# Experts 3 to 5 of a mixture of experts: the second product by seven block products, and its scaled additions and scatters moved into the next expert

## The chip, the cores and the metric

One core of a Trainium2 chip runs the whole program. The metric is the time of one execution on the device, in microseconds. The kernel before takes 1454.23 us, the median of three runs (1453.94 to 1454.76).

The engines have short names in the profile: PE is TensorE (PEld its weight loads), DVE is VectorE, ACT is ScalarE, POOL is GpSimd, SP is SyncE, which here issues DMAs.

## What is computed

The program is two transformer layers on 4096 tokens of width 256: gated attention in groups, a low-rank feed-forward, an attention with relu weights, and a mixture of experts. The change touches only the last. There, eight experts each choose their 1024 best tokens, and a token's output is the sum over the experts that chose it:

```
S = sigmoid(xt @ Wg).T
G, I = top_k(S, k)                       # 8 experts, k = 1024 tokens each
ex = xt[I]                               # gathered rows, 1024 x 256 per expert
hid = gelu(einsum('ekh,ehf->ekf', ex, W1) + b1)       # 1024 x 1024
out = (einsum('ekf,efh->ekh', hid, W2) + b2) * G[..., None]   # 1024 x 256
new_x = zeros.at[I].add(out)             # scattered back and added
```

The result then goes through a layer norm and is added to x. All is float32.

## The kernel before

The mixture of experts is a loop over 16 units `u` (line 2388), two for each expert `e`: `q` = 0 and 1 are the first and second 512 of its 1024 tokens. A unit's rows come as four gathered tiles of 128 tokens (`lists[e].got`), which TensorE transposes in `turn` into `xT[u]`, with the features in the partitions. The order of instructions on TensorE, VectorE and ScalarE is the program's own order (a manual schedule); on GpSimd it is left to the scheduler up to expert 5 and is the program's own from expert 6 on.

**The two ways to the hidden layer.** Experts 0, 1, 2 and 7 use `feed_forward`, once per unit: eight blocks of 128 hidden features, each two matmuls of 512 columns. Experts 3 to 6 (`by_seven`) use `feed_forward_by_seven`, both units at once. The 1024 tokens and the 1024 hidden features are each halved, and the product of 2 x 2 blocks is made from seven block products instead of eight (Strassen's method in Winograd's form). The loop over `f` runs over four chunks, each with seven matmuls of 512 columns into four banks named a to d, all under the tag "mm" with five banks. VectorE adds the partial products up in `u2`, `c22`, `c21` and `c12`, and four gelus of ScalarE write `hid`. The sums of weight blocks that these products need are made by `weight_sums` on GpSimd (four subtractions or additions of 128x512), those of tokens by `token_sums` on VectorE.

**The second product.** `project_back(u, hid)` makes a unit's four output tiles. For each, eight matmuls of 256 columns sum over the hidden features in a bank `py` (tag "y", two banks); then VectorE adds the bias and multiplies by the gates (lines 2332, 2333) and GpSimd scatters the tile with an adding indirect DMA into `acc_d` in DRAM (line 2334). The tile `y` has seven buffers. The scatters of an expert wait for all those of the expert before.

**What is fitted in between.** `turns_within(u)` says which transposes and token sums for the next units go behind which tile of `project_back`. Before an expert by seven, all transposes of both its units stand in the last unit of the expert before, behind tiles 0, 1 and 2.

The lists of chosen tokens for later experts are made beside all this. `agenda` holds their steps in order: for each list sort, rank, chunks, two steps of places, collect and gather. `go_on_with_lists(u, time, within)` is called at set points; it takes one step if the time booked for the last ones has run out and `u` is far enough, and with `within` only a step that has no TensorE work. `rank`, `chunks` and `places` are rows of small VectorE operations (lines 1916 to 1971); `gather` ends in eight row fetches on GpSimd (`got`, line 2005).

**The end.** In expert 6, `fetch_last` fetches the rows of the last expert's tokens into `xg` (eight more fetches), ahead of expert 6's second product in GpSimd's order. At the start of expert 7 `begin_last` reads `acc_d` back as soon as all scatters are done, and expert 7's units carry the last layer norm in `aside`, by a table (`beside_last`): statistics on VectorE, scaling on ScalarE, stores, and at the very end the final scatters of the chosen rows (line 2110). Its second products are added by line 2328.

Room that serves twice in the change: `wq1`, `wk1`, `wv` are the weights of the attention before, no longer needed here; `accg` and `xg` belong to expert 7.

Of the kernel before, what the change touches and what calls it, by code (L numbers as in the profile page):

```python
# [9 lines left out]
F32 = mybir.dt.float32  # L10
# [3 lines left out]
AF = mybir.ActivationFunctionType  # L14
ALU = mybir.AluOpType
# [4 lines left out]
P = 128  # L20
D = 256
DC = D // P
TB = 512
NJ = TB // P
# [13 lines left out]
FC = DFF // P  # L38
# [7 lines left out]
NE = 8  # L46
# [28 lines left out]
def kernel(  # L75
# [32 lines left out]
    nc = tc.nc  # L108
    B, S, _ = x_in.shape
    NT = B * S  # L110
# [1644 lines left out]
    with ExitStack() as st4:  # L1755
# [409 lines left out]
        QPE = NC // NJ  # L2165
        xT = {}

        def turn(u, c, half=None):

            if c == 0 and not half:  # L2170
                xT[u] = wk.tile([P, DC, TB], F32, tag="xT", name="xT")
            e, q = divmod(u, QPE)
            tiles = range(NJ) if half is None else range(half * NJ // 2, (half + 1) * NJ // 2)
            tp = ps.tile([P, NJ, P], F32, tag="mm", name="tp", bufs=5)
            for i in tiles:
                nc.tensor.transpose(tp[:, i, :], lists[e].got[q * NJ + i][:, c * P : (c + 1) * P], ident)
# [4 lines left out]
            copy = nc.scalar.copy if by_seven(e) else nc.vector.tensor_copy  # L2181
            copy(xT[u][:, c, cols], tp.rearrange("p j t -> p (j t)")[:, cols])  # L2182

        def by_seven(e):

            return 3 <= e < NE - 1

        rooms = [x.rearrange("p j d -> p (j d)")[:, h * TB : (h + 1) * TB] for x in xs[:4] for h in range(2)]
        seven = dict(zip(("sum0", "T1", "sum1", "T2", "T4", "S1", "S2", "S4"), rooms))
# [13 lines left out]
        def token_sums(e, n):  # L2203

            (b11, b21), (b12, b22) = ([xT[QPE * e + q][:, c, :] for c in range(DC)] for q in range(QPE))
            t1, t2, t4 = (seven[name] for name in ("T1", "T2", "T4"))
            dst, x, y = ((t1, b12, b11), (t2, b22, t1), (b12, b22, b12), (t4, b21, t2))[n]
            nc.vector.tensor_tensor(dst, x, y, ALU.subtract)

        def turns_within(u):  # L2210

            e, q = divmod(u, QPE)
            if u == QPE * NE - 1:
                return {}
            turns = {c: (lambda c=c: turn(u + 1, c)) for c in range(DC)}
            if q == QPE - 1 and by_seven(e + 1):
                both = [
                    turns[0], turns[1], lambda: turn(u + 2, 0), lambda: token_sums(e + 1, 0), lambda: turn(u + 2, 1),
                    *(lambda n=n: token_sums(e + 1, n) for n in (1, 2, 3)),
                ]  # L2220
                return {0: both[0:1], 1: both[1:4], 2: both[4:]}
            if by_seven(e) and q == 0:
                return {}
            return {2: [turns[0], turns[1]]} if u == 1 else {1: [turns[0]], 2: [turns[1]]}

        def feed_forward_by_seven(e):

            w1, w2 = weights[e]
            hid = [wk.tile([P, FC, TB], F32, tag="hid", name="hid") for _ in range(QPE)]
            (b11, b21), (t3, b22) = ([xT[QPE * e + q][:, c, :] for c in range(DC)] for q in range(QPE))  # L2230
            t1, t2, t4 = (seven[name] for name in ("T1", "T2", "T4"))
            half = DFF // 2
            s3 = w1[:, 0, half:DFF]
            s1, s2, s4 = (seven[name] for name in ("S1", "S2", "S4"))

            def product(bank, a, b, start, stop, f):
                nc.tensor.matmul(bank, lhsT=a[:, f * P : (f + 1) * P], rhs=b, start=start, stop=stop, skip_group_check=not start)  # L2237

            gelus = []

            def gelu(n, f, src):
                gelus.append(nc.scalar.activation(hid[n][:, f, :], src, AF.Gelu, bias=mb1[:, e * FC + f : e * FC + f + 1]))

            HC = FC // 2
            for f in range(HC):
                a, b, c, d = (ps.tile([P, TB], F32, tag="mm", name=f"ph{k}", bufs=5) for k in range(4))
# [5 lines left out]
                nc.vector.tensor_tensor(u2, u2, b, ALU.add)  # L2252
                product(c, s3, t3, True, True, f)
                nc.vector.tensor_tensor(c22, u2, c, ALU.add)
                product(d, s1, t1, True, True, f)
                nc.vector.tensor_tensor(c22, c22, d, ALU.add)
                product(a, w1[:, 1, 0:half], b21, False, True, f)
                gelu(0, f, a)
                if f < HC - 1:
                    go_on_with_lists(QPE * e, 3.2, True)  # L2260
                gelu(1, HC + f, c22)
                product(c, w1[:, 1, half:DFF], t4, False, True, f)
                nc.vector.tensor_tensor(c21, u2, c, ALU.add)
                gelu(0, HC + f, c21)
                product(d, s4, b22, False, True, f)
                nc.vector.tensor_tensor(c12, u2, d, ALU.add)
                gelu(1, f, c12)
                go_on_with_lists(QPE * e, 3.0)
            for q in range(QPE):
                if q == 0 and by_seven(e + 1):  # L2270
                    weight_sums(e + 1, gelus[-1])
                if q == 0 and e == NE - 2:
                    fetch_last()
                project_back(QPE * e + q, hid[q])

        def feed_forward(u):
            e, q = divmod(u, QPE)
# [30 lines left out]
        def project_back(u, hid):  # L2308

            e, q = divmod(u, QPE)  # L2310
            w1, w2 = weights[e]
            ahead = turns_within(u)
            for i in range(NJ):
                k = q * NJ + i
                py = ps.tile([P, D], F32, tag="y", name="py")
                for f in range(FC):
                    nc.tensor.matmul(  # L2317
                        py,
                        lhsT=hid[:, f, i * P : (i + 1) * P],
                        rhs=w2[:, f, :],  # L2320
                        start=(f == 0),
                        stop=(f == FC - 1),
                    )
# [9 lines left out]
                nc.vector.tensor_scalar(y, y, gates, None, ALU.mult)  # L2333
                scatter = nc.gpsimd.indirect_dma_start(  # L2334
                    out=acc_d[:, :],
                    out_offset=lists[e].at_chunk(k),
                    in_=y,
                    in_offset=None,
                    bounds_check=NT - 1,
                    oob_is_err=True,  # L2340
                    compute_op=ALU.add,
                )
# [91 lines left out]
```

## Time and profile before

The profiled execution took 1461.5 us; its span, from first to last instruction, is 1459.7 us. Below are the busy times of its last stages, in us; TensorE's granted clock is a share of full speed.

| stage (us from the start) | length | PE | DVE | ACT | POOL | PE clock |
|---|---|---|---|---|---|---|
| expert 3, 1169.5 to 1224.6 | 55.1 | 55.1 | 33.8 | 15.3 | 25.8 | 1.00 |
| expert 4, 1224.6 to 1279.6 | 55.0 | 55.0 | 27.4 | 15.4 | 25.8 | 1.00 |
| expert 5, 1279.6 to 1334.7 | 55.1 | 55.1 | 27.5 | 15.4 | 25.8 | 1.00 |
| expert 6, 1334.7 to 1393.8 | 59.1 | 56.0 | 24.1 | 13.2 | 30.4 | 0.97 |
| expert 7 and the end, 1393.8 to 1459.7 | 65.9 | 56.1 | 38.2 | 26.9 | 37.7 | 0.94 |

How to read it: TensorE's ends are modelled, so a busy TensorE need not be at its peak; what counts is whether it ever waits. A row of a timeline gives the start, the busy time, the engine, the line, the operation, its output and inputs, their shapes, and in brackets the idle time before it with what ended it. Each float32 matmul appears as two records, each with its own weight load.

### The profile page before, as it was taken

Reading aid. Unit: us, or ns where it says so; the run is one execution under the profiler, and the core shown is the slowest. Engines: PE = TensorE matmul, PEld = TensorE weight load, DVE = VectorE, ACT = ScalarE, POOL = GpSimd, SP = SyncE. Lnnn points to the kernel's source line nnn. Section 1 sums busy time; section 2 is a strip of 40 time slices with the busy share of each in tenths; the row PEclk is TensorE's granted clock in tenths of the full one; section 3 lists DMA queues with packets and bytes.
Section 4 is the critical chain, followed back from the end, with each engine's and each line's share of the span. In section 5 each row is a group of like instructions: output and inputs, shape, how many; then the busy total and the mean of one; then the engine's idle time right before and its main releaser. Section 6 shows DMA issues by size and latency. Waiting matters only on the chain.

```text
span 1459.7 us, 26465 instructions
## 1 busy us (share of the span) xinstructions
PE 1407.1 (96%) x10392; PEld 859.7 (59%) x10392; DVE 863.5 (59%) x2133; ACT 735.9 (50%) x1014; POOL 531.2 (36%) x662
## 2 busy tenths in 40 slices
PE   8999999999889999999999999949999999999997
PEld 4666666666644445454454547717666656756674
DVE  5457555666454637664757486885545766355246
ACT  4244454444368887878778788712221232232143
POOL 4123322322352223423333223413425325543655
PEclk9999999999999999999999999979999999999998
DMA  8400000001652373537244711152414223333365
GB/s 223 140 1 1 0 1 1 1 1 40 206 166 83 115 223 94 154 117 233 73 142 149 227 59 35 46 163 41 106 26 121 50 84 69 78 97 58 76 168 133
DMA packets 104853, 138.76 MB, mean 95 GB/s; under 512 B 25469, under 2 KB 64794, under 8 KB 104602
## 3 DMA queue, kind: packets, MB, share of 16 engines
q1 hardware_dynamic: 74512, 81.75, 18.2%
q0 software_dynamic: 30160, 55.32, 16.3%
q8 instruction: 81, 1.33, 0.4%
q14 instruction: 42, 0.34, 0.1%
q10 hardware_dynamic: 58, 0.01, 0.0%
HBM read 75.29 MB, written 61.51 MB: 94 GB/s over the span
## 4 chain that ended last, share of the span: by engine, by line
PE 86%; DVE 6%; issue 2%; DMA 2%; POOL 2%; ACT 1%; another core or an unknown queue 1%; SPq 0%; POOLq 0%; DVEq 0%; ACTq 0%
PE po L1553 16%; PE py L2317 14%; PE sc L1532 10%; PE ph L2237 7%; PE ph L2291 7%; PE pg L722 4%; PE pv L738 4%; PE py L848 3%; PE pt L1308 2%; PE pq L397 2%; PE po L820 2%; PE ph L904 2%; PE pv L431 2%; PE po L824 1%; PE pkv L835 1%
## 5 line engine op out<-in xcount | busy, mean ns | idle before, releaser
L1710 ACT ACTIVATE w<-sc 128x1024 f32<-128x1024 f32 x395 | 379.9, 1023 | 60.8 <-PE sc L1532 60.2
L1553 PE MATMUL po<-w,vaug 128*17 128x256 f32 (+1 forms) x4608 | 256.0, 358 | 1.5 <-DVE turned L1611 1.2
L2317 PE MATMUL py<-w,hid 128*128 128x256 f32 x1024 | 230.6, 382 | 3.1 <-DVE y L2332 3.1
L2317 PEld LDWEIGHTS py<-w,hid 128*128 128x128 f32 x1024 | 193.1, 191 | 33.5 <-issue 4.4
L1712 DVE TENSOR_SCALAR w<-sc 128x1024 f32<-128x1024 f32 x117 | 142.4, 1220 | 79.5 <-PE sc L1532 76.1
L1553 PEld LDWEIGHTS po<-w,vaug 128*17 128x17 f32 x4608 | 116.3, 97 | 118.0 <-issue 48.3
L1532 PE MATMUL sc<-q,kT 64*128 64x512 f32 (+1 forms) x1152 | 170.3, 404 | 2.5 <-ACT w L1710 1.3
L1532 PEld LDWEIGHTS sc<-q,kT 64*128 64x128 f32 x1152 | 89.9, 185 | 83.5 <-issue 46.7
L2334 POOL DMA_INDIRECT acc_d<-y,idx x56 | 88.1, 1574 | 119.8 <-DVE y L2333 59.5
L2298 ACT ACTIVATE hid<-ph,mb 128x512 f32<-128x512 f32 (+1 forms) x72 | 46.1, 640 | 164.8 <-PE ph L2291 137.2
L2291 PE MATMUL ph<-xT,w 128*128 128x512 f32 (+1 forms) x288 | 114.8, 552 | 0.3 <-DVE xT L2182 0.3
L2005 POOL DMA_INDIRECT got<-tok_d,idx x64 | 66.9, 1045 | 113.0 <-DVE idx L1995 96.0
L2291 PEld LDWEIGHTS ph<-xT,w 128*128 128x128 f32 x288 | 52.6, 190 | 51.3 <-issue 48.5
L371 POOL DMA_DIRECT2D kT<-k_d x32 | 23.4, 732 | 118.4 <-PE sc L1532 55.4
L2332 DVE TENSOR_TENSOR y<-py,mb 128x256 f32<-128x256 f32 x56 | 23.5, 420 | 71.8 <-PE py L2317 51.7
L722 PE MATMUL pg<-nT,wh 128*128 128x512 f32 x128 | 61.6, 613 | 1.5 <-ACT nT L661 1.5
L848 PE MATMUL py<-wo,oT 128*128 128x256 f32 x256 | 61.6, 384 | 0.0
L738 PE MATMUL pv<-wh,nT 128*128 128x512 f32 x128 | 59.7, 592 | 0.0
L848 PEld LDWEIGHTS py<-wo,oT 128*128 128x128 f32 x256 | 47.5, 190 | 17.6 <-issue 11.1
L746 ACT ACTIVATE v<-v 128x512 f32<-128x512 f32 x32 | 20.2, 630 | 62.7 <-DVE v L745 62.7
L1137 POOL TENSOR_TENSOR rsb<-veb,mhalf 128x1 f32<-128x1 f32 x30 | 19.6, 653 | 86.8 <-DVE veb L1136 86.8
L586 POOL TENSOR_TENSOR x<-x,y 128x1024 f32<-128x1024 f32 x13 | 30.6, 2355 | 56.3 <-ACT y L575 56.3
(352 smaller groups left out, 2338.0 us busy)
## 6 DMA issues: line engine op xcount, KB each, us to landing
q<-q_d POOLq DMA_DIRECT2D x16, 1024.0 KB
kT<-k_d POOLq DMA_DIRECT2D x32, 512.0 KB
w<-in_L_ffn_W_dram SPq DMA_DIRECT2D x16, 1024.0 KB
k_d<-parts SPq DMA_DIRECT2D x48, 256.0 KB
q_d<-parts SPq DMA_DIRECT2D x48, 256.0 KB
acc_d<-logits SPq DMA_DIRECT2D x8, 512.0 KB
tok_d<-hg SPq DMA_DIRECT2D x30, 128.0 KB
x<-in_L_attn_x_dram SPq DMA_DIRECT2D x7, 512.0 KB
```

The source lines that it names most:

```text
L722: nc.tensor.matmul(pg, lhsT=wh[:, c, HID + e * P : HID + (e + 1) * P], rhs=d["nT"][:, c, :], start=(c == 0), stop=(c == DC - 1),)
L738: nc.tensor.matmul(pv, lhsT=d["nT"][:, c, i * P : (i + 1) * P], rhs=wh[:, c, 0:HID], start=(c == 0), stop=(c == DC - 1),)
L848: nc.tensor.matmul(py, lhsT=d["oT"][:, e, :], rhs=wo[:, e, :], start=(e == 0), stop=(e == EC - 1))
L1532: nc.tensor.matmul(sc[:, j, m * n : (m + 1) * n], lhsT=row["kT"][t, r][rows, u, (kt + m) * P : (kt + m + 1) * P], rhs=row["q"][qh, t][rows ...
L1553: nc.tensor.matmul(po[rows : rows + HD + 1, at : at + n], lhsT=row["v"][:, kt + m, HQ * t + 4 * r + 2 * u + j, :], rhs=w[:, j, (2 * m + pa ...
L1710: nc.scalar.activation(w, sc, AF.Relu)
L1712: nc.vector.tensor_scalar(w, sc, 0.0, None, ALU.max)
L2005: return nc.gpsimd.indirect_dma_start(out=dst, out_offset=None, in_=rows[:, :], in_offset=self.at_chunk(c), bounds_check=NT - 1, oob_is_er ...
L2237: nc.tensor.matmul(bank, lhsT=a[:, f * P : (f + 1) * P], rhs=b, start=start, stop=stop, skip_group_check=not start)
L2291: nc.tensor.matmul(ph, lhsT=w1[:, c, f * P : (f + 1) * P], rhs=xT[u][:, c, h * n : (h + 1) * n], start=(c == 0), stop=(c == DC - 1),)
L2317: nc.tensor.matmul(py, lhsT=hid[:, f, i * P : (i + 1) * P], rhs=w2[:, f, :], start=(f == 0), stop=(f == FC - 1),)
L2334: scatter = nc.gpsimd.indirect_dma_start(out=acc_d[:, :], out_offset=lists[e].at_chunk(k), in_=y, in_offset=None, bounds_check=NT - 1, oob ...
```

## The change

`back_by_seven(e)` is true for experts 3, 4 and 5. For these, `project_back_by_seven` takes the place of both calls of `project_back`. It splits the 1024 tokens, the 1024 hidden features and the 256 outputs in halves and makes the second product from seven block products in five banks (p1, p4, p5, p6, p7; the second product on p1 and on p5 adds onto what is there). Each is 4 token tiles x 4 hidden blocks of matmuls with 128 columns, into one bank of tag "mm". The four sums of hidden blocks (s1 to s4, 128x2048 each) are made by VectorE; the four sums of W2's blocks by `back_sums` on GpSimd, behind chunk 0's last gelu of the same expert.

The bias times gate comes from ScalarE (`of_bias`); VectorE adds each gated half tile onto it (`add`). The first four half tiles are added at once; the other twelve half tiles' additions and all eight scatters go into `put_off`, twelve entries, of which six are taken at the end of each of the next expert's chunks. While `put_off` holds work the calls of `go_on_with_lists` in these chunks are left out. Within the second product three calls are left instead of eight.

The transposes for the next expert use the tag "y", whose banks are now 512 wide; `y` has nine buffers instead of seven.

```diff
-        def turn(u, c, half=None):
+        def turn(u, c, half=None, tag="mm"):
...
-            tp = ps.tile([P, NJ, P], F32, tag="mm", name="tp", bufs=5)
+            tp = ps.tile([P, NJ, P], F32, tag=tag, name="tp", bufs=5 if tag == "mm" else 2)
...
+        def back_by_seven(e):
+
+            return 3 <= e < NE - 2
...
-                if f < HC - 1:
+                if f < HC - 1 and (f > 1 or not put_off):
                     go_on_with_lists(QPE * e, 3.2, True)
...
-                go_on_with_lists(QPE * e, 3.0)
+                if f == 0 and back_by_seven(e):
+                    back_sums(e, gelus[-1])
+                if put_off:
+                    for _ in range(min(6, len(put_off))):
+                        put_off.pop(0)()
+                if not put_off:
+                    go_on_with_lists(QPE * e, 3.0)
+            if back_by_seven(e):
+                project_back_by_seven(e, hid)
+                return
...
+        def back_sums(e, behind):
+
+            (b11, b12), (b21, b22) = back_blocks(e)
+            t1, t2, t4 = (room.rearrange("p (f n) -> p f n", n=P) for room in back_rooms)
+            for dst, x, y in ((t1, b12, b11), (t2, b22, t1), (b12, b22, b12), (t4, b21, t2)):
+                after_all(nc.gpsimd.tensor_tensor(dst, x, y, ALU.subtract), [behind])
+
+        def project_back_by_seven(e, hid):
+
...
+            s1 = accg.rearrange("p k d -> p (k d)").rearrange("p (f t) -> p f t", t=TB)
+            s2, s3, s4 = a11, a21, a12
+            u2, v, c21, kept = (xg.rearrange("p k d -> p (k d)")[:, n * TB : (n + 1) * TB] for n in range(4))
+            ahead = turns_within(QPE * e + 1)
...
+            def lists_too(if_by_seven):
+                if not by_seven(e):
+                    go_on_with_lists(QPE * e + 1, 0.35)
+                elif if_by_seven:
+                    go_on_with_lists(QPE * e + 1, 3.5)
+
+            def product(bank, a, b, start, stop):
+                for i in range(NJ):
+                    for f in range(HC):
+                        nc.tensor.matmul(
+                            bank[:, i * P : (i + 1) * P],
+                            lhsT=a[:, f, i * P : (i + 1) * P],
+                            rhs=b[:, f, :],
...
+            def of_bias(q):
+                for k in range(q * NJ, (q + 1) * NJ):
+                    ys[k] = wk.tile([P, D], F32, tag="y", name="y", bufs=9)
+                    nc.scalar.activation(ys[k], mb2[:, e, :], AF.Identity, scale=gates[k])
+
+            def add(k, n, src):
+                i = k % NJ
+                y = ys[k][:, n * P : (n + 1) * P]
+                nc.vector.scalar_tensor_tensor(y, src[:, i * P : (i + 1) * P], gates[k], y, ALU.mult, ALU.add)
...
+            p1 = new_bank("p1")
+            product(p1, a11, b11, True, True)
+            nc.scalar.copy(u2, p1)
+            nc.vector.tensor_tensor(s1, a21, a22, plus)
+            nc.vector.tensor_tensor(s3, a11, a21, sub)
...
+            p4 = new_bank("p4")
+            product(p4, a22, t4, True, True)
+            nc.vector.tensor_tensor(s2, s1, a11, sub)
...
+            product(p1, a12, b21, False, True)
+            of_bias(0)
+            for k in range(NJ):
+                add(k, 0, p1)
+            summed_up = nc.vector.tensor_tensor(s4, a12, s2, sub)
+            if by_seven(e + 1):
+                weight_sums(e + 1, summed_up)
+            lists_too(True)
+            for do in ahead.get(0, ()):
+                do()
+            p5 = new_bank("p5")
+            product(p5, s1, t1, True, True)
+            nc.scalar.copy(kept, p5)
+            for do in ahead.get(1, ()):
+                do()
+            lists_too(True)
+            p6 = new_bank("p6")
+            product(p6, s2, t2, True, True)
+            nc.vector.tensor_tensor(u2, u2, p6, plus)
+            of_bias(1)
+            for do in ahead.get(2, ()):
+                do()
+            lists_too(True)
+            p7 = new_bank("p7")
+            product(p7, s3, t3, True, True)
+            nc.vector.tensor_tensor(v, u2, p7, plus)
+            nc.vector.tensor_tensor(c21, v, p4, plus)
+            nc.vector.tensor_tensor(v, v, kept, plus)
+            for k in range(NJ, NC):
+                put_off.append(lambda k=k: add(k, 0, c21))
+                put_off.append(lambda k=k: (add(k, 1, v), put(k)))
+            lists_too(False)
+            product(p5, s4, b22, False, True)
+            nc.vector.tensor_tensor(u2, u2, p5, plus)
+            put_off.extend(lambda k=k: (add(k, 1, u2), put(k)) for k in range(NJ))
...
-                py = ps.tile([P, D], F32, tag="y", name="py")
+                py = ps.tile([P, TB], F32, tag="y", name="py")[:, 0:D]
...
-                y = wk.tile([P, D], F32, tag="y", name="y", bufs=7)
+                y = wk.tile([P, D], F32, tag="y", name="y", bufs=9)
```

Here `a11` to `a22` are the halves of `hid` (first index tokens, second hidden features), `b11` to `b22` those of W2, `t1`, `t2`, `t4` the sums in `back_rooms` and `t3` the one that overwrites `b12`; `put(k)` is the scatter of tile k, as in `project_back`.

More of the change, by code (lines that the diff above doesn't have):

```diff
@@ L2180, in turn @@
             cols = slice(tiles[0] * P, (tiles[-1] + 1) * P)
-            copy = nc.scalar.copy if by_seven(e) else nc.vector.tensor_copy
+            copy = nc.scalar.copy if by_seven(e) or back_by_seven(e) else nc.vector.tensor_copy
             copy(xT[u][:, c, cols], tp.rearrange("p j t -> p (j t)")[:, cols])
@@ L2214, in turns_within @@
                 return {}
-            turns = {c: (lambda c=c: turn(u + 1, c)) for c in range(DC)}
+            tag = "y" if back_by_seven(e) else "mm"
+            turns = {c: (lambda c=c: turn(u + 1, c, tag=tag)) for c in range(DC)}
             if q == QPE - 1 and by_seven(e + 1):
                 both = [
-                    turns[0], turns[1], lambda: turn(u + 2, 0), lambda: token_sums(e + 1, 0), lambda: turn(u + 2, 1),
+                    turns[0], turns[1], lambda: turn(u + 2, 0, tag=tag), lambda: token_sums(e + 1, 0),
+                    lambda: turn(u + 2, 1, tag=tag),
                     *(lambda n=n: token_sums(e + 1, n) for n in (1, 2, 3)),
@@ L2221, in turns_within @@
                 return {0: both[0:1], 1: both[1:4], 2: both[4:]}
-            if by_seven(e) and q == 0:
+            if (by_seven(e) or back_by_seven(e)) and q == 0:
                 return {}
@@ L2274, in feed_forward_by_seven, with back_blocks @@
                 project_back(QPE * e + q, hid[q])
+        put_off = []
+        back_rooms = [x.rearrange("p c d -> p (c d)") for x in (wq1, wk1, wv)]
+        def back_blocks(e):
+            w2 = weights[e][1]
+            return [[w2[:, h * FC // 2 : (h + 1) * FC // 2, n * P : (n + 1) * P] for n in range(2)] for h in range(2)]
+        def back_sums(e, behind):
[3 more added lines that the diff above has]
+                after_all(nc.gpsimd.tensor_tensor(dst, x, y, ALU.subtract), [behind])
@@ new lines, in project_back_by_seven, with new_bank, put @@
+        def project_back_by_seven(e, hid):
+            (b11, t3), (b21, b22) = back_blocks(e)
+            t1, t2, t4 = (room.rearrange("p (f n) -> p f n", n=P) for room in back_rooms)
+            HC = FC // 2
+            (a11, a12), (a21, a22) = ([hid[q][:, h * HC : (h + 1) * HC, :] for h in range(2)] for q in range(QPE))
+            s1 = accg.rearrange("p k d -> p (k d)").rearrange("p (f t) -> p f t", t=TB)
+            s2, s3, s4 = a11, a21, a12
+            u2, v, c21, kept = (xg.rearrange("p k d -> p (k d)")[:, n * TB : (n + 1) * TB] for n in range(4))
+            ahead = turns_within(QPE * e + 1)
+            gates = [lists[e].got[k][:, D + e : D + e + 1] for k in range(NC)]
+            ys = {}
+            def new_bank(name):
+                return ps.tile([P, TB], F32, tag="mm", name=name, bufs=5)
+            def lists_too(if_by_seven):
[10 more added lines that the diff above has]
+                            rhs=b[:, f, :],
+                            start=start and not i and not f,
+                            stop=stop and f == HC - 1,
+                            skip_group_check=True,
+                        )
+            def of_bias(q):
[6 more added lines that the diff above has]
+                nc.vector.scalar_tensor_tensor(y, src[:, i * P : (i + 1) * P], gates[k], y, ALU.mult, ALU.add)
+            def put(k):
+                scatter = nc.gpsimd.indirect_dma_start(
+                    out=acc_d[:, :],
+                    out_offset=lists[e].at_chunk(k),
+                    in_=ys[k],
+                    in_offset=None,
+                    bounds_check=NT - 1,
+                    oob_is_err=True,
+                    compute_op=ALU.add,
+                )
+                after_all(scatter, scattered[e - 1] if e else ())
+                beside_each_other(scatter, scattered[e])
+            sub, plus = ALU.subtract, ALU.add
+            p1 = new_bank("p1")
[7 more added lines that the diff above has]
+            nc.vector.tensor_tensor(s2, s1, a11, sub)
+            lists_too(False)
+            product(p1, a12, b21, False, True)
[29 more added lines that the diff above has]
+                put_off.append(lambda k=k: (add(k, 1, v), put(k)))
+            lists_too(False)
+            product(p5, s4, b22, False, True)
+            nc.vector.tensor_tensor(u2, u2, p5, plus)
+            put_off.extend(lambda k=k: (add(k, 1, u2), put(k)) for k in range(NJ))
+            lists_too(False)
```

## The prediction

> **What bounds the kernel now.** I read the page's first part, then the TensorE timeline of experts 3 to 6, then the other engines' timelines at the places where the change works.
>
> ```profile
> PE 1407.1 (96%) x10392; PEld 859.7 (59%) x10392; DVE 863.5 (59%) x2133; ACT 735.9 (50%) x1014; POOL 531.2 (36%) x662
> ```
>
> TensorE sets the time. Its timeline (start, duration, engine, line, operation, output and inputs, count) shows expert 4's second product:
>
> ```profile
> 1250.07 17.43 PE L2317 MATMUL py<-w,hid 128*128 128x256 f32 x80
> 1267.34 0.60 PE L2176 MATMUL tp<-ident,got 128*128 128x128 f32 x4
> 1267.78 3.62 PE L2317 MATMUL py<-w,hid 128*128 128x256 f32 x16
> ```
>
> No idle bracket: 80 matmuls in 17.27 us, 0.216 us each. Experts 3, 4 and 5 take 55 us each, TensorE busy throughout. A matmul saved is time saved, and a wait added is time lost.
>
> **The product itself.** The 64 matmuls of an expert are 128 records (the page has x1024 for eight experts), 128 x 0.216 = 27.6 us. Seven products of 16 matmuls are 224 records with 128 columns. The nearest row has the same shape on both sides:
>
> ```profile
> 173.17 0.38 PE L820 MATMUL po<-packed,v 128*128 128x128 f32 x2
> 173.40 0.39 PE L824 MATMUL po<-head,kv 128*128 128x128 f32 x2
> ...
> 174.74 0.39 PE L824 MATMUL po<-head,kv 128*128 128x128 f32 x2
> 174.96 1.06 PE L688 MATMUL psim<-head,head 128*128 128x128 f32 x8
> ```
>
> From 173.17 to 174.96 lie 16 records, each with its own weight load: 0.112 us each. 224 x 0.112 = 25.1 us, so 2.5 us less per expert, **-7.6 us** for three. The Trainium skill (TensorE: Matmul & The Clock Gate, Back-to-back issue gap) speaks against this: in a stream of weight-load and matmul pairs the load is part of the spacing, about 81 ns at 128 columns against 56 for a matmul alone. Scaled by 1.45 a record would take 0.162 us, the product 36.3 us, and the change would lose 8.7 us per expert, 26 in all. The trace has the very pairs at 0.112, and I take the trace. Ends: 0.109 (transposes, 4 in 0.44 us) for -9.6 us, and 0.162.
>
> **What lies beside the products.** Count from the first of the seven. Each takes 3.58 us. VectorE gets four 128x2048 sums; 512 wide go at 0.61 us, 1024 wide at 1.14, so some 2.2 each: s1 is there at 3.9, s3 at 6.1, s2 at 8.4; p5 needs s1 at 11.2, p6 needs s2 at 15.7. s4, behind the first four additions, is ready at 14.1 and wanted at 23.3. With five 128x512 additions (3.0) and 16 half-wide scaled ones (4.2) VectorE gets 16 us per expert and loses 8 x 0.77 = 6.2; it was busy 10.6 of 29.5 us here. ScalarE gets two copies (0.57) and eight Identity rows (0.5, the rate at L2071), 5.1 us, where it was busy 3.7 of 29.5. I cost these at nothing; TensorE hides them. Without that cover the sum needed next (2.2 us) would show. The transposes stay 16; they come earlier, at 10.7 and 15.2 instead of 17.3. In expert 3 the gather of rows already stands at the end of the first product: row fetches start 1.2 us behind it, one per 1.32 us, the last issued at 11.6, and DMA traffic of that burst is over by 13.1. Four rows are wanted at 10.7, eight at 15.2: two microseconds to spare, cost nothing; per microsecond later, one lost. The two py banks are as many as before; y's nine buffers hold eight rows and one more. The eight scatters (1.85 us each on GpSimd when they queue) move into the next expert's chunks: with back_sums' 5.6 us they fill GpSimd from about 7.5 to 28 us of experts 4 and 5, and the next row fetches begin at 27 to 28, so the margin above loses at most one. SyncE's weight loads wait for the same last readers as before.
>
> **Put-off additions.** In the first product a chunk takes 6.01 us, and its sixth matmul pair overwrites a bank that VectorE must have read. This is chunk 0 of expert 4:
>
> ```profile
> 1226.16 1.28 DVE L1971 TENSOR_TENSOR at<-lo,each 128x1024 bf16<-128x1024 bf16 x2
> 1227.36 0.68 DVE L2252 TENSOR_TENSOR x<-x,ph 128x512 f32<-128x512 f32 x1
> 1228.15 0.69 DVE L2254 TENSOR_TENSOR hid<-x,ph 128x512 f32<-128x512 f32 x1
> ```
>
> L2252 starts 2.8 us into the chunk, L2254 ends at 4.29, the pair starts at once. So VectorE may be free for L2252 as late as X = 2.8; later costs X - 2.8. A half-wide scaled addition is not in the trace. The same operation goes at 0.17 us for 32 columns and 0.395 for 256, on a line between 0.26 for 128; six are 1.6 us, behind the chunk's own last addition (ends at 0.8). Chunk 1: X = 2.4, no loss. At the end of chunk 1 `put_off` is empty and the list work starts again, 1.2 us of places: chunk 2 has X = 3.6, 0.85 us lost. Chunk 0 lost 0.25 before (6.26 us), and that goes. Net 0.6 in experts 4, 5, 6: **+1.8 us**. Ends: 0 and 4.
>
> **back_sums on GpSimd.** These are four more 128x512 sums per expert behind chunk 0's last gelu. The row to read is expert 2, where weight_sums ran beside VectorE's search:
>
> ```profile
> 1154.63 4.52 DVE L1824 TENSOR_TENSOR ge<-by_e,tried 128x224 bf16<-128x224 f32 x4
> ```
>
> ```profile
> 1154.70 1.45 POOL L2201 TENSOR_TENSOR x<-w 128x512 f32<-128x512 f32 x1 [12.81 <-ACT hid L2298]
> 1156.23 1.30 POOL L2201 TENSOR_TENSOR w<-w 128x512 f32<-128x512 f32 x1
> ```
>
> Elsewhere these four VectorE operations take 1.30 us (at 1151.09), here 4.52: each waits out one sum on GpSimd, some 1.4 us. Now chunk 1 of expert 3:
>
> ```profile
> 1177.11 0.25 DVE L1927 SCALAR_TENSOR_TENSOR chosen<-upto,room,kinds 128x32 f32<-128x32 f32 x1
> 1177.39 0.19 DVE L1928 TENSOR_TENSOR chosen<-chosen,kinds 128x32 f32<-128x32 f32 x1
> ...
> 1178.17 0.68 DVE L2252 TENSOR_TENSOR x<-x,ph 128x512 f32<-128x512 f32 x1
> ```
>
> ScalarE's second gelu ends at 1177.17, so back_sums starts at about 1177.3. Three or four small operations with both inputs in SBUF stand from L1928 on; each waits, and L2252 moves from 1178.17 to 1181.7 or 1182.8. L2254 ends 1.5 later; the sixth pair stood at 1179.95. That is 3.3 to 4.4 us; I take **+3.8**. Ends: 0 and 6, since the one gap of this length in the trace (3.13 us at 1370.7) was followed by a granted clock of 0.5 and cost 5.1 in all. In experts 4 and 5 the put-off additions meet the sums: if these go first, two additions wait and chunk 1 has X = 4.7, 2 us lost; if a scatter goes first, chunk 2 gets one to two such waits, 1 to 2.6. I take 1.7 each, **+3.4**; ends 0 and 8.
>
> **Lists later, and the tail.** While `put_off` holds work the list steps stand still; gather moves from the end of chunk 1 to the end of chunk 3, 12 us. In expert 6 GpSimd then has 16 fetches before the scatters. They stood like this:
>
> ```profile
> 1369.17 1.01 POOL L2005 DMA_INDIRECT xg<-x_d,idx  x1 [0.30 <-issue]
> 1370.48 1.62 POOL L2334 DMA_INDIRECT acc_d<-y,idx  x1 [0.30 <-issue]
> ...
> 1395.05 1.55 POOL L2334 DMA_INDIRECT acc_d<-y,idx  x1 [1.32 <-DVE y L2333]
> 1399.70 1.08 POOL L2005 DMA_INDIRECT accg<-acc_d,idx  x1 [3.09 <-DMA acc_d<-y,idx]
> ```
>
> From the first fetch (1349.29) to the first scatter are 21.2 us. Starting 1.2 us into the second product, scatters begin at 22.4; at 1.85 us each (the spacing at 1215 to 1221) the eighth is issued at 35.3. The product lasts 28.5, so that is 6.8 us into expert 7, where it was 1.3: 5.5 later. The read-back waits for it, then stats, scales, stores, the second read-backs (1418.7, 1421.7) and their stats (1427.48). From there to L2328 at 1439.58 VectorE has 12.1 us with 1.6 of idle, so L2328 comes 4 us late, and the final row of reciprocals and scatters on GpSimd, 1441.01 to 1454.8, has hardly a gap to catch up in. **+4.2**; ends 0 and 6.
>
> **Sum.** -7.6 + 1.8 + 3.8 + 3.4 + 4.2 = +5.6 us. The profiled execution took 1461.5 us (span 1459.7), 7.3 above the median of 1454.23; 5.1 of that is one stall of expert 6, where VectorE waited 7.65 us for something the trace calls remote. The change touches nothing that explains it, so I count it as the profile's own and add the sum to the median: **1459.8 us**.
>
> **Rivals.** First, the products alone come through: GpSimd's sums find other moments, and expert 7's slack takes the delay. For it: TensorE without one gap, and POOL busy 36%. Against it: the row of 4.52 us. -7.6 + 1.8 = 1448.4, or 1452.6 with the late tail. Second, the weight load sets the pace: +26 and the waits, 1480 or more; against it 16 pairs at 0.112, for it only that the longest such run in the trace is short. Third, the rows for the next expert land late and TensorE waits in all three: two microseconds of margin used up and 2 to 4 more lost each time, 1466 to 1472.
>
> **Numbers.** Forecast with its near values (1456 to 1465) 0.55; first rival 0.20; a sum near zero, where one of the three waits fails to appear, 0.14; the third rival 0.08; the weight load 0.03. A measurement tells 0.2% (2.9 us) from no change. Faster 0.20, same 0.14, slower 0.66. The range takes in most of the first rival and stops short of the second and most of the third: 1449 to 1467.
>
> **What would show it.** The new matmuls 0.11 us apart, 25 us for each expert's seven products; gaps of 3 to 4 us in chunk 1 of expert 3, of 1 to 2 in chunks 1 and 2 of experts 4 and 5; VectorE's small operations stretched over back_sums; the last scatter of expert 6 some 7 us into expert 7; L2328's row behind VectorE in the last half expert. I am wrong if VectorE and back_sums hardly meet, or if expert 7 ends as far behind expert 6 as before.

## The result and the profile after

The changed kernel takes **1477.83 us** (median of four runs, 1475.82 to 1483.25), the kernel before 1454.09 beside it (1452.92 to 1454.76): a ratio of 1.017, interval 1.0142 to 1.0198. It is 23.7 us slower, where 5.6 were forecast; the range ended at 1467. The page of the profile after has

```profile
PE 1405.3 (95%) x10680; PEld 862.7 (58%) x10680; DVE 908.2 (62%) x2160; ACT 749.4 (51%) x1044; POOL 566.2 (38%) x674
```

TensorE's busy time hardly changed (1407.1 before: fewer matmuls, some of them at a lower clock), though its span is 16.9 us longer: what came is mostly waiting. The view of waits, TensorE alone, from 1160 us to the end (what was waited for, us in total, times, longest) gives nearly all of it:

```profile
PE ph L2243 <- DVE hid L2260: 12.0, 4, 4.5
PE tp L2176 <- DMA got<-tok_d,idx: 6.5, 7, 1.2
...
```

Neither line existed before. The first is the first product waiting for VectorE, the second the transposes waiting for the next expert's rows. A table of stages, from the starts in TensorE's timeline, places them; the other rows are the experiments below ("first" and "second" are the two products of an expert, in us, for experts 3, 4, 5 and 6).

| kernel | first product, 3 / 4 / 5 / 6 | second product, 3 / 4 / 5 / 6 | median us | before, same chip | ratio (95%) |
|---|---|---|---|---|---|
| before | 25.4 / 25.5 / 25.6 / 25.5 | 29.6 / 29.5 / 29.5 / 33.6 | 1454.09 | | |
| after | 29.9 / 31.2 / 31.8 / 26.2 | 29.9 / 29.9 / 29.9 / 28.6 | 1477.83 | 1454.09 | 1.0170 (1.0142–1.0198) |
| vector_sums | 25.4 / 26.2 / 26.2 / 26.2 | 31.5 / 31.6 / 31.6 / 34.3 | 1467.92 | 1457.57 | 1.0072 (1.0054–1.0090) |
| lists_on_time | 29.8 / 30.5 / 30.6 / 26.3 | 29.9 / 26.9 / 26.9 / 31.8 | 1472.42 | 1457.57 | 1.0114 (1.0088–1.0141) |
| in_pieces | 28.2 / 31.6 / 31.6 / 26.2 | 27.0 / 27.0 / 27.2 / 35.6 | 1468.60 | 1457.57 | 1.0084 (1.0056–1.0113) |
| all_three | 25.4 / 26.3 / 26.3 / 26.3 | 28.7 / 26.9 / 26.9 / 33.4 | 1456.96 | 1457.57 | 0.9994 (0.9984–1.0005) |
| sums_late | 25.4 / 26.2 / 26.2 / 26.2 | 30.0 / 33.2 / 33.2 / 35.0 | 1470.67 | 1456.41 | 1.0097 (1.0076–1.0119) |
| late_gpsimd | 25.4 / 25.5 / 25.5 / 25.5 | 27.0 / 34.9 / 32.2 / 35.7 | 1467.14 | 1456.41 | 1.0067 (1.0052–1.0082) |
| spread_vector | 25.4 / 25.8 / 25.5 / 25.5 | 27.0 / 28.7 / 28.7 / 35.4 | 1458.24 | 1456.41 | 1.0001 (0.9991–1.0011) |
| three_nine | 25.4 / 25.5 / 25.5 / 25.5 | 27.0 / 28.7 / 27.5 / 36.8 | 1457.75 | 1460.19 | 0.9978 (0.9967–0.9988) |
| fetch_between | 25.4 / 25.5 / 25.5 / 25.5 | 27.0 / 27.5 / 27.6 / 28.5 | 1452.61 | 1460.19 | 0.9957 (0.9943–0.9970) |
| fetch_between_again | 25.4 / 25.5 / 25.5 / 25.5 | 27.0 / 27.5 / 28.6 / 28.5 | 1452.78 | 1454.35 | 0.9989 (0.9982–0.9996) |
| before_between | 25.4 / 25.5 / 25.5 / 25.5 | 29.6 / 29.5 / 29.5 / 28.5 | 1455.56 | 1454.35 | 1.0007 (0.9999–1.0016) |

The kernel before differs by about 6 us between chips, so times are compared within a row only. A stage without a wait repeats between profiles to a tenth; expert 6's second product does not, and is taken up at the end of the experiments.

**The first product of expert 3.** VectorE's timeline (start, us, engine, line, operation, operands) beside GpSimd's four new sums, as in the prediction's fence of before, where L1928 took 0.19 and L2252, now L2258, started at 1178.17:

```profile
1176.69 1.17 DVE L1928 TENSOR_TENSOR chosen<-chosen,kinds 128x32 f32<-128x32 f32 x1
1177.89 0.19 DVE L1931 SCALAR_TENSOR_TENSOR place<-place,chosen 128x32 f32<-128x32 f32 x1
1178.12 1.13 DVE L1933 TENSOR_SCALAR hi<-place 128x32 f32<-128x32 f32 x1
1179.28 1.20 DVE L1935 SCALAR_TENSOR_TENSOR lo<-hi,place 128x32 bf16<-128x32 f32 x1
1180.40 0.68 DVE L2258 TENSOR_TENSOR x<-x,ph 128x512 f32<-128x512 f32 x1
```

```profile
1176.55 1.26 POOL L2305 TENSOR_TENSOR wq<-w 128x512 f32<-128x512 f32 x1 [4.07 <-ACT hid L2248]
...
1180.39 1.26 POOL L2305 TENSOR_TENSOR wv<-w,wk 128x512 f32<-128x512 f32 x1
```

Three operations of 0.2 us each take 1.1 to 1.2, one for each of the first three sums. L2258, which reads PSUM, keeps its 0.68 us although the fourth sum runs beside it. This is the mechanism that the prediction expected here.

**The first product of expert 5.** Here the put-off additions meet the same sums. VectorE's and then GpSimd's timeline:

```profile
1296.50 1.66 DVE L2349 SCALAR_TENSOR_TENSOR y<-xg,got,y 128x128 f32<-128x128 f32 x6
...
1302.51 5.40 DVE L2349 SCALAR_TENSOR_TENSOR y<-xg,got,y 128x128 f32<-128x128 f32 x6
1307.82 1.28 DVE L1971 TENSOR_TENSOR at<-lo,each 128x1024 bf16<-128x1024 bf16 x2
1309.03 0.68 DVE L2258 TENSOR_TENSOR x<-x,ph 128x512 f32<-128x512 f32 x1
```

```profile
1301.13 1.57 POOL L2352 DMA_INDIRECT acc_d<-y,idx  x1 [0.17 <-issue]
1302.22 1.78 POOL L2305 TENSOR_TENSOR wk<-w,wq 128x512 f32<-128x512 f32 x1
1303.45 1.76 POOL L2305 TENSOR_TENSOR w<-w 128x512 f32<-128x512 f32 x1
1304.67 1.75 POOL L2305 TENSOR_TENSOR wv<-w,wk 128x512 f32<-128x512 f32 x1
```

Six additions take 1.66 us in chunk 0 and 5.40 in chunk 1: 3.74 us more for three sums, 1.25 each. A scatter, gated by the additions, stands between the first sum and the other three, so these three move out of chunk 1's middle to the end of its work on VectorE, just where the second six additions are. Then a list step (1.28) follows, and L2258 starts 7.3 us into chunk 2 (1301.70) instead of the 2.8 it can afford. TensorE's timeline shows what that costs:

```profile
1305.13 1.02 PE L2243 MATMUL ph<-xT,w 128*128 128x512 f32 x2
1310.55 2.08 PE L2243 MATMUL ph<-x,w 128*128 128x512 f32 x2 [4.40 <-DVE hid L2260]
1312.42 1.91 PE L2243 MATMUL ph<-xT,x 128*128 128x512 f32 x2
...
1315.30 1.13 PE L2243 MATMUL ph<-xT,w 128*128 128x512 f32 x2
```

4.40 us of waiting, and then two pairs 1.87 and 1.84 us apart instead of 0.86 and 0.95: the granted clock of this stage is 0.89. The gap costs another 1.9 us after it is over.

**The seven products.** TensorE's timeline in expert 3:

```profile
1198.71 3.82 PE L2332 MATMUL p<-w,hid 128*128 128x128 f32 x32
1202.36 3.74 PE L2332 MATMUL p<-wv,hid 128*128 128x128 f32 x32
...
1210.26 3.74 PE L2332 MATMUL p<-wq,accg 128*128 128x128 f32 x32
1213.84 0.82 PE L2176 MATMUL tp<-ident,got 128*128 128x128 f32 x6
1215.86 0.33 PE L2176 MATMUL tp<-ident,got 128*128 128x128 f32 x1 [1.21 <-DMA got<-tok_d,idx]
1217.19 0.33 PE L2176 MATMUL tp<-ident,got 128*128 128x128 f32 x1 [1.00 <-DMA got<-tok_d,idx]
```

A product is 32 records in 3.57 to 3.65 us, 0.112 each: the row at L820 carried over. But the second eight transposes, 0.9 us of work, last from 1213.84 to 1217.35. GpSimd's fetches of those rows, and VectorE's sums of hidden blocks beside them:

```profile
1201.33 2.27 POOL L2005 DMA_INDIRECT got<-tok_d,idx  x1 [0.31 <-issue]
1203.89 1.97 POOL L2005 DMA_INDIRECT got<-tok_d,idx  x1 [0.30 <-issue]
1206.17 2.09 POOL L2005 DMA_INDIRECT got<-tok_d,idx  x1 [0.30 <-issue]
1208.56 1.01 POOL L2005 DMA_INDIRECT got<-tok_d,idx  x1 [0.30 <-issue]
...
1211.19 2.79 POOL L2005 DMA_INDIRECT got<-tok_d,idx  x1 [0.30 <-issue]
```

```profile
1200.36 2.29 DVE L2368 TENSOR_TENSOR accg<-hid 128x2048 f32<-128x2048 f32 x1 [0.71 <-ACT hid L2248]
1202.68 2.29 DVE L2369 TENSOR_TENSOR hid<-hid 128x2048 f32<-128x2048 f32 x1
1205.08 2.29 DVE L2373 TENSOR_TENSOR hid<-accg,hid 128x2048 f32<-128x2048 f32 x1
...
1210.82 2.28 DVE L2379 TENSOR_TENSOR hid<-hid 128x2048 f32<-128x2048 f32 x1
```

A fetch with no wide sum beside it takes 1.01 us. The four long ones end 0.95, 0.89, 0.89 and 0.88 us after the end of the sum that ran when they began (1203.60 against 1202.65, and so on): they stand still for the sum and then take their usual time. So the lock works both ways. The last fetch is issued at 1214.29, 15.6 us after the first product's end, where the prediction had 11.6.

**Expert 6 and the tail.** GpSimd's timeline, with expert 7 beginning at 1406.12:

```profile
1399.94 1.62 POOL L2470 DMA_INDIRECT acc_d<-y,idx  x1 [0.30 <-DVE xT L2182]
...
1413.00 1.55 POOL L2470 DMA_INDIRECT acc_d<-y,idx  x1 [0.31 <-issue]
1417.63 1.08 POOL L2005 DMA_INDIRECT accg<-acc_d,idx  x1 [3.07 <-DMA acc_d<-y,idx]
```

The last scatter is issued 6.9 us into expert 7 (forecast 6.8). Expert 7 takes 58.0 us instead of 56.1, and 12.6 us instead of 9.8 follow TensorE's last matmul.

### The profile page after: what moved, and what is told of

The parts are those of the page before. It is cut to its first block, busy times and chain, and to the rows that moved or that the text cites. A ratio compares the mean times of both kernels' runs of the same rounds, so it can differ in the third digit from the quotient of the medians.

```text
span 1476.6 us, 27151 instructions
## 1 busy us (share of the span) xinstructions
PE 1405.3 (95%) x10680; PEld 862.7 (58%) x10680; DVE 908.2 (62%) x2160; ACT 749.4 (51%) x1044; POOL 566.2 (38%) x674
## 4 chain that ended last, share of the span: by engine, by line
PE 80%; DVE 7%; issue 4%; DMA 4%; POOL 3%; ACT 1%; SPq 0%; POOLq 0%; ACTq 0%; DVEq 0%
PE po L1553 15%; PE sc L1532 10%; PE py L2453 7%; PE ph L2243 6%; PE ph L2427 6%; PE p L2332 4%; PE pg L722 4%; PE pv L738 4%; PE py L848 3%; PE pt L1308 2%; PE pq L397 2%; PE po L820 2%; PE ph L904 2%; PE pv L431 2%; PE po L824 1%
## 5 line engine op out<-in xcount | busy, mean ns | idle before, releaser
L1710 ACT ACTIVATE w<-sc 128x1024 f32<-128x1024 f32 x395 | 379.9, 1024 | 60.7 <-PE sc L1532 60.0
L2453 PE MATMUL py<-w,hid 128*128 128x256 f32 x640 | 143.9, 381 | 1.3 <-ACT hid L2434 0.7
L2453 PEld LDWEIGHTS py<-w,hid 128*128 128x128 f32 x640 | 119.6, 190 | 20.7 <-issue 3.0
L2005 POOL DMA_INDIRECT got<-tok_d,idx x64 | 82.0, 1281 | 87.2 <-DVE idx L1995 70.1
L586 POOL TENSOR_TENSOR x<-x,y 128x1024 f32<-128x1024 f32 x13 | 30.6, 2355 | 56.3 <-ACT y L575 56.3
```

The costliest lines, as they stand in the source:

```text
L1710: nc.scalar.activation(w, sc, AF.Relu)
L2005: return nc.gpsimd.indirect_dma_start(out=dst, out_offset=None, in_=rows[:, :], in_offset=self.at_chunk(c), bounds_check=NT - 1, oob_is_er ...
L2453: nc.tensor.matmul(py, lhsT=hid[:, f, i * P : (i + 1) * P], rhs=w2[:, f, :], start=(f == 0), stop=(f == FC - 1),)
```

## The experiments

**Theory**: GpSimd and VectorE keep each other out whenever both work on SBUF alone. GpSimd's four sums stop VectorE in the first product; VectorE's four wide sums stop the row fetches in the second. **Rival**: VectorE has simply too much to do, and the rows are late because their gather was moved.

**vector_sums**, the sums of W2's blocks on the other engine:

```diff
-                if f == 0 and back_by_seven(e):
-                    back_sums(e, gelus[-1])
...
             if back_by_seven(e):
+                back_sums(e)
                 project_back_by_seven(e, hid)
...
-            for dst, x, y in ((t1, b12, b11), (t2, b22, t1), (b12, b22, b12), (t4, b21, t2)):
-                after_all(nc.gpsimd.tensor_tensor(dst, x, y, ALU.subtract), [behind])
+            for dst, x, y in ((t1, b12, b11), (t2, b22, t1), (t4, b21, t2), (b12, b22, b12)):
+                nc.vector.tensor_tensor(dst, x, y, ALU.subtract)
```

> The four sums of W2's blocks (back_sums) go from GpSimd, behind chunk 0's last gelu, to VectorE, ahead of the seven products. Theory (the sums on GpSimd hold off VectorE's operations that read and write only SBUF): the first products of experts 3, 4 and 5, now 29.9, 31.2 and 31.8 us, return to 25.5 to 26.2 us, no gap of over 1 us stays in them, and the whole falls by 14 to 16 us, to about 1463. Rival (VectorE simply has too much to do once the put-off additions are there): the gap in expert 3 goes, 4.4 us, since nothing is put off there; the gaps of 4.5 us in chunk 2 of experts 4 and 5 stay; about 1473.

The first products fell to 25.4, 26.2 and 26.2 us. VectorE does the same additions and more, so the rival falls: sums on GpSimd cost 4.5, 5.0 and 5.6 us, and the put-off additions by themselves 0.7 us (one gap of 0.66 in chunk 2). TensorE's waits in this profile:

```profile
PE tp L2176 <- DMA got<-tok_d,idx: 7.3, 6, 1.5
PE py L2452 <- DVE y L2467: 3.8, 1, 3.8
PE ph L2243 <- DVE hid L2260: 2.0, 3, 0.7
```

The time stayed above the forecast. The second products take 1.6 us more each: their waits for rows grew by only 0.3 us each (the last fetch is issued 15.6 us in, as in the change), but behind each pair of waits the granted clock fell to 0.50 for 3.4 us, where it had stayed at 1.00. And expert 6 has a wait of its own.

**lists_on_time**, the list steps no longer held back:

```diff
-                if f < HC - 1 and (f > 1 or not put_off):
+                if f < HC - 1:
...
-                if not put_off:
-                    go_on_with_lists(QPE * e, 3.0)
+                go_on_with_lists(QPE * e, 3.0)
```

> The list steps are no longer held back while put-off additions are left. Theory (the late gather is what costs the seven products their gain in experts 4 and 5, and what lengthens the tail): the rows of experts 5 and 6 are fetched during the first product, the transposes' waits (2.1 us and a slow stretch, 2.9 in all) stay in expert 3 and go in 4 and 5: -6; the tail -3 to -4; the list steps in chunks 0 and 1 give 1 to 3 back: 1468 to 1471. Rival (VectorE is the bound in these chunks): the steps meet GpSimd's sums together with the put-off additions and each waits its 1.3 us: what is won is lost, 1477 or more.

The second products of experts 4 and 5 fell by 3.0 us to 26.9, expert 3's stayed, and expert 7 is back at 56.1. The first products gained 0.7 and 1.2. As the theory had it, one or two microseconds above its range. (The slow stretch that it counts in expert 3 is not there: the granted clock of the change's second products is 1.00.) In experts 4 and 5 three fetches each still meet wide sums (1.9 to 2.1 us), but the gather starts earlier and its last fetch is issued 11.2 us in, in time.

**in_pieces**, the same sums cut in four:

```diff
+            def in_pieces(dst, x, y, op):
+                for f in range(HC):
+                    last = nc.vector.tensor_tensor(dst[:, f, :], x[:, f, :], y[:, f, :], op)
+                return last
...
-            nc.vector.tensor_tensor(s1, a21, a22, plus)
+            in_pieces(s1, a21, a22, plus)
```

and so for s2, s3 and s4.

> The four sums of hidden blocks (s1 to s4) are made as four 128x512 pieces each instead of one 128x2048 operation. Theory (a fetch on GpSimd waits for the end of VectorE's running operation, so fetches of 2.0 to 2.8 us are ones that met a sum of 2.3 us): with pieces of 0.6 to 0.7 us a fetch takes 1.0 to 1.6 us, the rows land 3 to 4 us earlier, the waits of 2.2 us at the transposes go in experts 3, 4 and 5; -6 to -9, about 1470. Rival (VectorE's operations back to back keep GpSimd out as long as they follow each other, whatever their length): the fetches stay as long as the four pieces together, no change.

GpSimd's fetches in expert 3:

```profile
1197.04 1.46 POOL L2005 DMA_INDIRECT got<-tok_d,idx  x1 [0.31 <-issue]
1198.80 1.45 POOL L2005 DMA_INDIRECT got<-tok_d,idx  x1 [0.30 <-issue]
1200.56 1.50 POOL L2005 DMA_INDIRECT got<-tok_d,idx  x1 [0.31 <-issue]
1202.37 1.01 POOL L2005 DMA_INDIRECT got<-tok_d,idx  x1 [0.30 <-issue]
```

About 1.5 instead of 2.0 to 2.3; the last fetch is issued 12.1 us in instead of 15.6, and no transpose waits. The seven products take 27.0 us in all three experts, with gathers still late: a late gather costs nothing where the fetches do not meet wide sums, and in lists_on_time meeting them cost nothing where the gather was early. (A first piece also needs only the first hidden blocks, so the sums start some 0.8 us earlier; that is part of the gain. Another 1.7 us of the time, in expert 3's first product, belong to the clock and not to the pieces; see the last section.)

**all_three** joins these edits.

> Sums of W2's blocks on VectorE, list steps on time and sums of hidden blocks in pieces, together. If the three causes are what they seem and do not overlap: -15 for the gaps, -9 for the rows, -3 for the tail, some of it back for the list steps: 1450 to 1453, at or just under the kernel before. If VectorE is then the bound in chunks 0 and 1 of experts 4 to 6 (12 additions, list steps and the sums): gaps of 1 to 3 us there, 1455 to 1465.

It came level with before. Expert 3's rows are again late (28.7) because four sums of W2's blocks now precede the wide ones, and 0.8 us stay in each first product of experts 4 to 6 (a gap of 0.66, now in chunk 1, where the list step stands).

**sums_late** asks if it is the place: the sums stay on GpSimd, behind chunk 2.

```diff
-                if f == 0 and back_by_seven(e):
+                if f == HC - 2 and back_by_seven(e):
```

> Of the change, one thing is altered: back_sums stays on GpSimd but stands behind chunk 2's last gelu instead of chunk 0's. VectorE has then only operations that read PSUM, and no list step and no put-off addition beside it. Theory (GpSimd's sums hold off only VectorE's operations that have all operands in SBUF; it is the place and not the amount of work): first products of experts 3, 4, 5 at 25.5, 26.2 and 26.2 us without a gap of over 1 us, seven products at 29.9 as in the change, 1463 to 1468 or 0.7 to 0.8% above before. Rival (GpSimd's sums slow any work of VectorE, or the first wide sum of hidden blocks, which would now meet them): the 5 us come back in chunk 3 or at the fifth product, 1475 to 1480.

Both halves came true, and the time lies between the two. The first products are those of vector_sums, with the sums on GpSimd, so the place decides. But the sums now meet the first wide sum of VectorE. TensorE's waits have

```profile
PE p L2332 <- POOL wv L2305: 3.3, 2, 1.7
```

and GpSimd's timeline in expert 4 shows T4's sum at 3.30 us instead of 1.26:

```profile
1249.85 3.30 POOL L2305 TENSOR_TENSOR wv<-w,wk 128x512 f32<-128x512 f32 x1
1253.31 2.96 POOL L2005 DMA_INDIRECT got<-tok_d,idx  x1 [0.16 <-issue]
```

The second product waits for its weights and then for its rows: 33.2 us.

**Towards a better version.** late_gpsimd joins sums_late, lists_on_time, in_pieces and another pace of the put-off entries; spread_vector does so with VectorE's sums at three places.

```diff
-                    for _ in range(min(6, len(put_off))):
+                    for _ in range(min((3, 7, 2, 0)[f], len(put_off))):
```

> back_sums on GpSimd behind chunk 2, list steps on time, sums of hidden blocks in pieces, and the put-off entries taken 3, 7 and 2 in chunks 0, 1 and 2 instead of 6 and 6. Theory: the 0.66 us gap in the first products of experts 4 to 6 goes (chunk 0 has 0.8 us less), first products 25.5 to 25.7, seven products 26.9 to 27.1 in all three experts; about 4 us under the version with the three causes taken out, 0.2 to 0.4% under before. Rival: in experts 4 and 5 the scatters (until 7 us into chunks 2 and 3) push the sums into the second product, p4 waits for its weights; no better than before.

> The same with the sums of W2's blocks on VectorE, two in chunk 2, one at the start of the second product, one behind s2. Theory: as the one with the sums on GpSimd behind chunk 2, first products 25.5 to 25.8, seven products 26.9 to 27.1, also in expert 3, where with all four sums ahead of s1 the rows were 1.5 us late; 0.2 to 0.4% under before. Rival: the two sums in chunk 2 make it late (VectorE free 2.9 us into chunk 3), a gap of 0.5 us instead; the gain stays at 0.1%.

The first products came to 25.5 us in both (25.8 once): with three additions instead of six in chunk 0 the 0.66 us gap is gone. On GpSimd the rival held, T4 was late by 3.0 us twice. On VectorE expert 3 was cured (27.0), but in experts 4 and 5 the fetches, which stand behind the scatters, start 27.6 us into the expert, where all_three had 25.2, and the rows come 1.3 to 1.6 us late; the time is level with before, short of what was expected. three_nine takes 3 and 9 entries; fetch_between also moves fetch_last:

```diff
-                if q == 0 and e == NE - 2:
+                if q == 1 and e == NE - 2:
                     fetch_last()
```

> As the last version on VectorE, but the put-off entries are taken 3 and 9, in chunks 0 and 1 alone. Theory (GpSimd issues in order, and there the scatters of chunk 2 stood ahead of the row fetches): scatters are over before the fetches again, rows in time, seven products 26.9 to 27.0 in experts 3, 4 and 5; first products 25.5 to 26.0 in experts 4 to 6; the profile from expert 3 to the start of expert 6's second product 4 to 5 us shorter than in the first version with all three causes taken out; 0.1 to 0.4% under before. Rival (what is won here is lost again in expert 6's second product, where the profiles show a wait of VectorE that none of the causes explains): the time stays at before's.

> The same, with the eight fetches of the last expert's rows (fetch_last) between expert 6's first and last four scatters instead of ahead of all eight. If the wait of VectorE in expert 6's second product (2 to 4 us in the profiles of the versions, none in the change's) comes from sixteen fetches in a row: it goes, expert 6's second product takes 28.5 us, 2 to 3 us less than the version before it, 0.3 to 0.5% under before. If not: the same time as that version, the wait at another tile.

three_nine came 0.22% under before, within its forecast, but kept a wait for rows of 1.5 us in expert 4 and 0.3 in expert 5, and its expert 6 stalled for 5.2 us. In fetch_between that stall is gone, and TensorE waits for almost nothing after 1140 us:

```profile
PE py L2460 <- ACT hid L2441: 0.7, 1, 0.7
PE py L2460 <- DVE accg L2471: 0.5, 1, 0.5
PE tp L2176 <- DMA got<-tok_d,idx: 0.4, 1, 0.4
...
```

How much of its 0.43% belongs to the order of the fetches? The kernel before got the same one-line edit, and ran on the same chip as the best version again:

> The kernel before with one line changed: the eight fetches of the last expert's rows between expert 6's first and last four scatters. If expert 6's wait of VectorE belongs to the sixteen fetches in a row in the kernel before too: its second product takes 28.5 us instead of 33.6, and the time falls by 2 to 5 us below before (less where before had no such wait in its runs). The tail is longer (VectorE and ScalarE of expert 7 as in the change) by 1 to 3 us. If the wait has another cause: within 0.1% of before.

> The best version once more, beside the kernel before with the same order of fetches. If the seven products are what wins: 5 to 7 us under that one (2.6 us in each second product of three experts, less 0 to 1.5 for late rows). If the order of the fetches is the gain: the same as that one within 0.1%.

Expert 6's second product is 28.5 us in before_between's profile instead of 33.6, with expert 7 and the tail unchanged (56.1 and 9.8 us, where 1 to 3 more were expected), yet the median is no better than before's. So the kernel before hardly had such a stall in its timed runs on that chip, only in the profile on record; on the chip where it took 1460 it may have had it, which these times cannot show. Against before_between the best version takes 2.8 us less (1452.78 against 1455.56), under the 5 to 7 expected: in its profile the 7.7 us of the three second products are nearly all taken back, by late rows in experts 4 and 5 (0.5 and 1.7 us) and a longer end (expert 7 58.8 us instead of 56.1, then 11.9 instead of 9.8). That execution, 1455.5 us, was the slowest of 21, so most give back less. The best version stands 0.1 to 0.4% under before, by chip.

Left open: what VectorE waits for in expert 6. In the profile of before the trace calls it remote. A stall there is in the profile of before and of all versions with sixteen fetches in a row, except that of the change itself, and in none of the three with four scatters among the fetches. That fits a cause in those fetches and does not show one.

## Why the prediction was wrong

Against the 16.9 us between the spans stand these terms, forecast and then measured from the table of stages.

- **Seven products, -7.6**: -7.7 (27.0 us in in_pieces against 29.6, 29.5, 29.5). Right: the records are 0.112 us apart, and the rival of the weight load, which gave 26 us, came near the total by accident and is refuted at its own place.
- **What lies beside the products, 0**: measured **+8.7** (29.9 us three times, against 27.0 in in_pieces). This step failed. VectorE's wide sums were costed by their own readiness, which held, and the fetches by the spacing of 1.32 us that they have in the kernel before, where VectorE works 0.8 us in each 3.45 beside them. That the two would run at the same time was not asked, though the next part of the prediction used the same lock in the other direction. The third rival named the outcome, without this mechanism, at 0.08.
- **Put-off additions, +1.8**: +2.1 (0.7 each in experts 4, 5, 6, from vector_sums). Right, and where it was forecast: a gap of 0.66 us in chunk 2, against 0.85.
- **back_sums in expert 3, +3.8**: +4.5. The three waits are right, the nearness of the sum is partly luck: the sixth pair came 2.7 us late, under the 3.3 to 4.4 forecast, and 1.8 of a slow clock, which the sum did not hold, came on top. In in_pieces the same gap was followed by no slow clock and cost 2.8.
- **back_sums in experts 4 and 5, 1.7 each**: measured **5.0 and 5.6**, 7.1 more in all. The order was the one named second, a scatter first, but it was counted as one to two waits. It is three: all sums but the first are pushed together into the second six additions. And no clock was counted after the gap, though the stall at 1370.7 in the profile of before had shown it: 1.3 and 1.9 us of the two.
- **The tail, +4.2**: +4.6 (expert 7 +1.8, the end +2.8). L2328's row came 3.2 us late, against 4. Only part is shown to be the late scatters': where they were on time again (1.3 us into expert 7, in lists_on_time and seven others), expert 7 was back at 56.1, but 10.7 to 11.9 us still followed TensorE's last matmul, instead of 9.8. What lengthens the end there is open.
- **Expert 6's stall**, counted as the profile's own: it is absent after (-5.0 us), and so the medians differ by more than the spans. Taking the median as base was right.

Without the last these terms sum to +22.8; the spans give 16.9 + 5.0 + 0.7 = 22.6 (0.7 because expert 3 starts earlier), the medians 23.7. The two failed terms, 8.7 and 7.1, are 15.8 of the 18 us by which the forecast missed.

The Trainium skill (SBUF — State Buffer, SBUF: two separate sides) has a lock of this kind: the port pair that VectorE and GpSimd share is held for a whole instruction, and GpSimd cannot write a DMA's descriptors while VectorE holds it. The page tells the second half only of 2-port operations such as a float32 copy, so it would not by itself have foretold the first failed term. Here float32 additions of two SBUF operands hold up a fetch as well, which ends 0.9 us after the sum; the measurement decides. That L2258 kept its 0.68 us beside a sum on GpSimd agrees with the page, which names two SBUF inputs.

## What to carry to other kernels

When work is moved to VectorE with all operands in SBUF, list what GpSimd does in the same microseconds, DMA issues included, and the other way round: each meeting costs the waiter the rest of the other's instruction, so wide operations cost most and pieces cost less. Count the meetings after the move, in each queue's real order; a scatter in between had gathered three sums into one place. A gap of TensorE can also cost in the clock behind it, 1.3 to 1.9 us each in this change, but not every gap did, and its length alone did not tell which.

## What was not expected

After the gaps of 2.5 and 4.4 us in experts 3 and 5 four records took 3.3 and 3.7 us instead of 1.7; after that of 4.5 us in expert 4 only the second pair was slow. With the records behind them 1.8, 1.9 and 1.3 us were lost. But in_pieces has the same gap in expert 3, and there the clock stays full. TensorE's timelines of the change and of in_pieces:

```profile
1181.92 1.83 PE L2243 MATMUL ph<-x,w 128*128 128x512 f32 x2 [2.51 <-DVE hid L2260]
1183.55 1.91 PE L2243 MATMUL ph<-xT,x 128*128 128x512 f32 x2
```

```profile
1179.12 1.12 PE L2243 MATMUL ph<-x,w 128*128 128x512 f32 x2 [2.51 <-DVE hid L2260]
1180.08 1.02 PE L2243 MATMUL ph<-xT,x 128*128 128x512 f32 x2
```

So the first product takes 28.2 us in in_pieces and not 29.9. A gap of 2.98 us in late_gpsimd (expert 4) had no slow clock behind it either, while in vector_sums two waits of 1.4 to 1.5 and 0.9 to 1.1 us, close together, had one in all three experts. From expert 3 to the last matmul the slow stretches of a profile last 3.41 us or twice that, and start multiples of 3.41 us apart (1182.20, 1250.47 and 1308.50 us in the change). On that grid the gap of 2.51 us lies inside one step in the change and is split into 1.0 and 1.5 in in_pieces; the one of 2.98 is split into 1.8 and 1.2. That fits a clock which is set step by step from the idle time in a step, and does not show it.

Pieces of 0.6 us let most fetches through in about 1.5 us, not after the one piece that was running: the pieces follow each other without a pause. Beside the four pieces of s4 the last fetch of a gather took 2.1 to 2.8 us in all_three (expert 3), spread_vector (4 and 5), three_nine (4) and fetch_between_again (5), about as long as beside one wide sum, and 1.04 in three_nine (5) and fetch_between_again (4). In the first group the rows came 1.3 to 1.6 us late, in the second 0.3 to 0.4, so this fetch makes most of what is left of the late rows. How GpSimd gets in between the pieces was not settled.
